# One product for values and ranks' scores, another layout of the dispatch table, and an earlier sum of the last chunk

## The chip, the cores and the metric

The kernel runs on one core of a Trainium2 chip. The metric is the time of one execution on the device in microseconds (us). The kernel before was run three times: 2809.46, 2814.0 and 2821.68 us, median 2814.0. One further execution was profiled.

The engines are TensorE (PE: matmuls, with weight loads listed apart as PEld), VectorE (DVE), ScalarE (ACT), GpSimd (POOL) and SyncE (SP), which issues most of the DMAs. GpSimd issues the indirect ones.

## The reference, cut to what matters

The input has 8 x 256 = 2048 tokens of 512 numbers, all in float32. Two layers follow each other:

```python
xn = _layernorm(x)
x = x + _L0_attn_ref(xn, ...) + _L0_ffn_ref(xn, ...)
xn = _layernorm(x)
x = x + _L1_attn_ref(xn, ...) + _L1_ffn_ref(xn, ...)
```

- `_L0_attn_ref` is linear attention with decay: 32 heads of 128, silu on queries, keys and values, causal within each sequence of 256. The heads' outputs are normalised together by their root mean square over all 32 x 128 numbers of a token, scaled by `norm_w`, multiplied by a sigmoid gate and projected to 512.
- `_L0_ffn_ref` is a mixture of 16 experts of width 128. A router picks two groups of four experts and then two experts for each token. A shared expert of width 256 is added for every token.
- `_L1_attn_ref` is softmax attention with a single head of 128: `q, k, v = x @ Wqkv + bqkv`, then a projection `Wo` with bias.
- `_L1_ffn_ref` is a low-rank mixture: `scores = x @ Wr.T` over 64 adapters of rank 16, the top 16 kept with softmax gates, `h = A x`, each rank multiplied by its adapter's gate, then `B h`, scaled by 2.

## The kernel before, in words

**Tiling.** Tokens are worked on in NCH = 4 chunks of CH = 512, each of TPC = 4 tiles of P = 128 tokens. The 512 channels are NC = 4 blocks of 128 partitions. Transposed operands have channels on the partitions. Every matmul here is in float32, and the profile counts two TensorE records for one. The large products use a seven-product scheme for 2x2 blocks in place of eight; the names `p1` to `p7` are its products.

**Opening.** Chunk by chunk, tokens are normalised (`Normal`, L251 to L258), transposed on TensorE (`turn_rows`, L278), and multiplied with the shared expert's weights (`shared_up`, L357). In `shared_up` a call of `between()` after each of the four projections computes the router's scores of one tile (`scores`, L313, 16 columns). Then `route` picks the experts on VectorE. Once all chunks are routed, the dispatch (L523 to L571) works out for each token and each of its two experts a slot number: the experts' tokens stand in NMT = 47 tiles of 128 slots, each tile belonging to one expert. `slots` holds the slot numbers, `own_` and `rows_` the expert of each tile.

**First layer.** Three loops: chunk i, group g (8 groups of four heads), and the outer product p in the order p1, p2, p6, p5, p3, p7, p4. Each outer product has seven inner ones of four matmuls (`product`, L731), 49 inner products in a group, and a group takes about 73 us. After each inner product `slot()` runs what is due of a list of `pieces`, such as scores of attention, projections and experts; `later(n, f)` puts a piece n slots ahead. ScalarE and GpSimd keep the program's order here; the other engines' instructions are ordered by the framework's planner, which takes the earliest in the program among those that its own model of the chip holds for ready. `tc.keep_in_program_order(ins)` pins an instruction behind all that its engine was given before. In chunk 0 weights are summed for the seven products: raw blocks are loaded (`st`, L674, from the pool `stage` of two buffers, tag `xw`) and added on VectorE and GpSimd, and the sums are stored in `ws` (L694). Later chunks load them (L705 to L708). For p1, p2 and p4 (`RAW`) block 0 of the weights is loaded as well, but `sums_of` uses only blocks 1 to 7.

**Experts.** In chunk 0 `scatter` (L1194) writes each token's number, 16 times in 64 bytes, to its slot of `table` in DRAM. In the last group of chunk 0, after 4 slots, `read_table` (L1203) loads the table into a buffer of `stage` with 47 partitions, one for each tile of slots. `turn_table`, 36 slots later, picks every 16th number, turns 47x128 to 128x47 on TensorE and writes `whose`. From chunk 1 on, `Expert(j)` gathers by column j of `whose` the tokens of tile j.

**Sums of squares.** `attend` adds the squares of two heads side by side into `sums` (two halves of S = 256 columns per sequence) on GpSimd. At a chunk's end `done` takes the column sums over partitions with matmuls against `ones` (`squares`, L1033): two for each tile, one for each half. `means` gives the factor `all_rms`; `finish` (L642) adds the attention's accumulator times this factor to the residual sum on VectorE. For chunks 0 to 2 this residual (shared expert and input, `xr`, with the experts' bias added by `last_bias` on GpSimd) is loaded by `load_sum`, and the result is stored in `xs_` by `store`.

**Second layer.** Before it begins, `wrapped_up` adds chunk 0's expert outputs (`gather`, L604, and `settle`, L615). Its loop over i runs two `low_rank` calls (L1601, seven products each) and one seven-product scheme with `B` (L1701). Python lists under the keys 1, 2, 7, 5, 3, 4 (`fill1`, `fill2`, `fill`) say which other work follows which product. In `fill1` and `fill2` the next chunk's sum is loaded (`next_x`), settled and normalised. In `fill` the next chunk's `Head` works: `route` (ranks, L1457, 64 columns, then the choice of 16 on VectorE), `qk` (L1453), `values` (L1520, 128 columns), `softmax` and `gates`. `gates` stores the chosen gates in DRAM, and `spread` (L1572) loads them back, repeated for each rank. Chunk 0's `Head` has an opening of its own, which puts the ranks between the matmuls of queries and keys (L1457, L1476). For chunk 3, `next_x` loads `xr` itself, adds the bias on GpSimd, and the third iteration (i = 2) runs `finish` in `fill1` under keys 2 and 7. A tile of the second layer that is asked for with `spare8()` comes from the pool `stage`.

## Time and profile before

| | |
|---|---|
| median of 3 runs | 2814.0 us (2809.46 to 2821.68) |
| the profiled execution | 2815.0 us |
| its span, first to last instruction | 2813.1 us |
| mean granted TensorE clock | 0.993 of full |
| TensorE busy | 2752.4 us, 98% of the span |
| VectorE, ScalarE, GpSimd busy | 1630.7, 947.6, 1645.8 us |
| moved by DMA | 752.66 MB, mean 268 GB/s |

A line of a timeline gives start and duration in us, engine, line of the kernel, operation, output<-inputs and shape; in brackets stands how long the engine was idle before and what it waited for. A line of waits gives the total in us, how many times, and the longest. A line of the chain (the work that ended last, followed back) gives start, duration and what ran. Engines with a q (SPq) are the issuing sides. Lines with L100 come from a helper for all additions, so tile names tell them apart. TensorE's granted clock falls to 0.5 of full at times. By the trace the first chunk of the first layer begins near 120 us and ends near 707, the later ones take about 585 us each, and the second layer begins near 2507.

### The profile page before, as it was taken

The page shows a single profiled execution, that of the slowest core. Times are in us where ns is not written, and L with a number is a line of the kernel's source. Part 1 is how long each engine was busy: PE and PEld are TensorE (multiplying, and loading weights), DVE is VectorE, ACT ScalarE, POOL GpSimd, SP SyncE. Part 2 cuts the span into 40 slices and gives each one's busy share as a digit, 9 for nine tenths or more (in the row PEclk, how much of TensorE's full clock was granted, in tenths as well). Part 3 has the DMA queues.
Part 4 walks back from the last instruction along what each step waited for, and adds up shares of the span by engine and source line. Part 5 has one row for each costly group of instructions (what it writes and reads, how often), then busy time and mean ns, then how long its engine had stood idle before and what let it go on. Part 6 is the DMA issues. An engine that isn't in the chain of part 4 may idle for free.

```text
span 2813.1 us, 49529 instructions
## 1 busy us (share of the span) xinstructions
PE 2752.4 (98%) x19653; PEld 2538.8 (90%) x19653; DVE 1630.7 (58%) x2722; ACT 947.6 (34%) x1683; POOL 1645.8 (59%) x1414
## 2 busy tenths in 40 slices
PE   9999999998999999999999999999999999999999
PEld 5699999998989999999999999999999999987877
DVE  7666777776445555555545555555455555656663
ACT  4232222221433333333343333333433333432211
POOL 6467777775566676666755555556555567642220
PEclk9999999999999999999999999999999999999999
DMA  7888888887977877778877777787777788662211
GB/s 276 322 339 337 319 330 329 322 317 293 346 273 288 290 288 273 288 277 299 316 264 261 261 271 261 264 311 279 282 271 265 270 312 305 221 222 77 68 55 62
DMA packets 155062, 752.66 MB, mean 268 GB/s; under 512 B 18721, under 2 KB 25249, under 8 KB 103457
## 3 DMA queue, kind: packets, MB, share of 16 engines
q1 hardware_dynamic: 136672, 678.67, 64.7%
q0 software_dynamic: 17872, 70.32, 7.6%
q8 instruction: 155, 2.54, 0.3%
q14 instruction: 75, 0.61, 0.1%
q10 hardware_dynamic: 288, 0.52, 0.1%
HBM read 605.66 MB, written 142.99 MB: 266 GB/s over the span
## 4 chain that ended last, share of the span: by engine, by line
PE 85%; DVE 6%; DMA 4%; issue 2%; POOL 2%; ACT 1%; another core or an unknown queue 0%; SPq 0%; DVEq 0%; POOLq 0%; ACTq 0%
PE ps_a L731 25%; PE ps_e L731 12%; PE ps_sc L942 10%; PE ps_b L731 7%; PE ps_o L865 4%; PE ps_sc L962 3%; PE ps_sc L853 3%; PE ps_sc L800 3%; PE ps_a L1601 2%; PE ps_o L866 2%; PE ps_sc L854 2%; PE ps_a L1701 2%; DMA st<-in_w_att_dram 2%; DVE w L100 1%; PE ps_sc L812 1%
## 5 line engine op out<-in xcount | busy, mean ns | idle before, releaser
L731 PE MATMUL ps_a<-xt,w 128*128 128x128 f32 x5376 | 752.9, 276 | 17.2 <-DVE r L100 7.8
L731 PEld LDWEIGHTS ps_a<-xt,w 128*128 128x128 f32 x5376 | 687.8, 192 | 47.3 <-issue 14.1
L100 POOL TENSOR_TENSOR c<-c 128x512 f32<-128x512 f32 x240 | 305.5, 1288 | 268.9 <-DVE c L100 266.5
L1099 ACT COPY cp<-ps_a 128x512 f32<-128x512 f32 x384 | 224.3, 584 | 667.7 <-PE ps_a L731 642.3
L100 POOL TENSOR_TENSOR c<-c,r 128x512 f32<-128x512 f32 x264 | 346.3, 1334 | 166.7 <-DVE r L100 164.2
L731 PE MATMUL ps_e<-xt,w 128*128 128x128 f32 x2688 | 374.8, 276 | 5.2 <-DVE c L100 1.6
L100 POOL TENSOR_TENSOR w<-w 128x512 f32<-128x512 f32 x224 | 298.2, 1339 | 93.2 <-DVE w L100 44.7
L731 PEld LDWEIGHTS ps_e<-xt,w 128*128 128x128 f32 x2688 | 341.3, 192 | 12.1 <-issue 4.8
L731 PE MATMUL ps_a<-w,xt 128*128 128x128 f32 x1792 | 346.9, 275 | 0.0
L100 POOL TENSOR_TENSOR sums<-sums,sq 128x512 f32<-128x512 f32 x120 | 155.9, 1299 | 280.9 <-ACT sq L880 280.4
L942 PE MATMUL ps_sc<-wo,gT 128*128 128x256 f32 x1288 | 304.9, 380 | 2.4 <-POOL gT L100 2.4
L731 PEld LDWEIGHTS ps_a<-w,xt 128*128 128x128 f32 x1792 | 272.6, 192 | 0.0
L942 PEld LDWEIGHTS ps_sc<-wo,gT 128*128 128x128 f32 x1288 | 232.9, 190 | 30.5 <-issue 2.9
L100 DVE TENSOR_TENSOR acc<-ps_sc,acc 128x512 f32<-128x512 f32 x208 | 142.6, 689 | 192.6 <-PE ps_sc L942 151.1
L885 DVE SCALAR_TENSOR_TENSOR gT<-ps_o,nw,c 128x256 f32<-128x256 f32 x256 | 111.9, 478 | 214.9 <-ACT sq L880 205.9
L731 PE MATMUL ps_b<-xt,w 128*128 128x128 f32 x1536 | 216.0, 277 | 13.1 <-DVE w L100 6.2
L100 DVE TENSOR_TENSOR c<-ps_a,c 128x512 f32<-128x512 f32 x216 | 146.8, 687 | 123.3 <-PE ps_a L731 118.5
L731 PEld LDWEIGHTS ps_b<-xt,w 128*128 128x128 f32 x1536 | 196.1, 194 | 16.0 <-issue 12.6
L828 ACT ACTIVATE c<-c 128x512 f32<-128x512 f32 x256 | 150.4, 628 | 145.8 <-DVE c L100 127.0
L880 ACT ACTIVATE sq<-ps_o 128x512 f32<-128x512 f32 x120 | 71.7, 597 | 367.0 <-PE ps_o L866 359.5
L100 DVE TENSOR_TENSOR s<-ps_sc,decay 128x384 f32<-128x384 f32 x256 | 139.5, 553 | 81.5 <-PE ps_sc L854 76.8
L731 PE MATMUL ps_e<-w,xt 128*128 128x128 f32 x896 | 173.5, 275 | 0.0
(306 smaller groups left out, 4747.4 us busy)
## 6 DMA issues: line engine op xcount, KB each, us to landing
w<-in_w_att_dram SPq DMA_DIRECT2D x128, 1024.0 KB
st<-in_w_att_dram SPq DMA_DIRECT2D x32, 1024.0 KB
wo<-in_w_out_dram SPq DMA_DIRECT2D x113, 256.0 KB
decay<-dec SPq DMA_DIRECT2D x64, 384.0 KB
w<-ws0p SPq DMA_DIRECT2D x12, 1792.0 KB
w<-ws1p SPq DMA_DIRECT2D x12, 1792.0 KB
w<-ws2p SPq DMA_DIRECT2D x12, 1792.0 KB
w<-ws3p SPq DMA_DIRECT2D x12, 1792.0 KB
```

Of the source, the lines that this page charges most:

```text
L100: (eng or nc.vector).tensor_tensor(o, a, b, op)
L731: mm(bank[:, bass.ts(ty, P)], a, b, start=(first and ty == 0), stop=True, skip_group_check=True,)
L800: mm(pu[:, bass.ts(n, P)], w12[:, n, c, :], self.xeT[:, c, :], start=(c == 0), stop=(c == NC - 1),)
L828: nc.scalar.activation(qk, qk, AF.Silu)
L853: mm(p[:, 0:S], self.c[:, 2 * hh, P : 2 * P], q, start=True, stop=True)
L854: mm(p[:, S : S + P], self.c[:, 2 * hh + 1, P : 2 * P], q[:, 1, :], start=True, stop=True,)
L865: mm(po[:, bass.ts(hh, S)], v[:, 0, :], self.s[:, hh, 0:S], start=True, stop=False)
L880: nc.scalar.activation(sq, po, AF.Square)
L885: nc.vector.scalar_tensor_tensor(gT[:, h, :].rearrange("p (t n) -> p t n", t=2), po[:, bass.ts(h, S)].rearrange("p (t n) -> p t n", t=2), ...
L942: mm(py[:, bass.ts(t, S)], self.O[p][:, hh, bass.ts(t, P)], self.wo[p][:, hh, :], start=(t == 0 and hh == 0), stop=(hh == 1), skip_group_c ...
L962: mm(py[:, bass.ts(h, S)], gT[:, hh, bass.ts(t, P)], self.wo[pair, h][:, hh, :], start=(h == 0 and hh == 0), stop=(hh == 1), skip_group_ch ...
L1099: nc.scalar.copy(c, bank)
```

## The change

- **Values and scores.** `fr` is joined to `wqkv` on the host. `Head.route` computes values (128 columns) and ranks' scores (64) as one product of 192 columns, in two halves of two tiles, each with a PSUM bank of its own. `values`, `opening` and `choose` go; chunk 0's head runs `route`, then `qk`.
- **Table by partitions.** A slot s is stored at row (s mod 128) * 47 + s / 128 (`places`, three VectorE operations in the dispatch), so that a partition's entries lie together. `read_table` reads 32 columns and later 15, into the buffer `sq`; `take_table` copies each half to `whose` 40 slots after its read, and starts the second read. The transpose goes. Both reads are pinned on SyncE's queue.
- **Squares.** In a chunk's last group GpSimd adds the two halves of `sums`; `squares` runs one matmul for a tile.
- **Last chunk's sum.** In i = 0, chunk 3's `xr` is loaded, gets its bias and its `finish` (without the pin), and is stored in `xs_`. `next_x` then loads `xs_` for every chunk.
- **Smaller parts.** In the second layer's `fill`, two of the next chunk's four `turn_rows` stand after the first product. RAW loads of later chunks take blocks 1 to 3. In the opening, the first of each tile's score matmuls of chunk 0 is pinned behind the projection before it.

```diff
-    def scores(pl, xT, t):
+    def scores(pl, xT, t, kept=lambda ins: ins):
         for c in range(NC):
-            mm(
+            ins = mm(
...
+            if c == 0:
+                kept(ins)
...
-        ups.append(shared_up(i, lambda: scores(pl, xT[i], tiles.pop(0))))
+        ups.append(shared_up(i, lambda: scores(pl, xT[i], tiles.pop(0), lambda ins: tc.keep_in_program_order(ins) if i == 0 else ins)))
...
+    whose = [const.tile([P, n], I32, name=f"whose{n}") for n in (READ, NMT - READ)]
...
+    nc.vector.tensor_scalar(tile_of, slots, 7, None, ALU.arith_shift_right)
+    nc.vector.tensor_scalar(places, slots, P - 1, None, ALU.bitwise_and)
+    nc.vector.scalar_tensor_tensor(places, places, float(NMT), tile_of, ALU.mult, ALU.add)
...
-                nc.sync.dma_start(out=y, in_=w_att[g, RAW[p]])
+                nc.sync.dma_start(out=w[:, 1:4], in_=w_att[g, RAW[p]][:, 1:4])
...
+                if u.g == NG - 1 and self.pair == 1:
+                    add(sums[:, 0:S], sums[:, 0:S], sums[:, S:], nc.gpsimd)
...
-                        for n in range(2):
-                            mm(
-                                pr[:, t : t + 1],
-                                sums_[i][:, t // 2, n * S + t % 2 * P : n * S + (t % 2 + 1) * P], ones,
-                                start=(n == 0), stop=(n == 1),
-                            )
+                        mm(
+                            pr[:, t : t + 1], sums_[i][:, t // 2, bass.ts(t % 2, P)], ones,
+                            start=True, stop=True,
+                        )
...
-                out_offset=bass.IndirectOffsetOnAxis(ap=slots[:, n, t : t + 1], axis=0),
+                out_offset=bass.IndirectOffsetOnAxis(ap=places[:, n, t : t + 1], axis=0),
...
-        def read_table():
-
-            rows = staged("rows")[0:NMT, 0 : P * SAME]
-            nc.sync.dma_start(out=rows, in_=table.rearrange("(j p) o -> j (p o)", p=P).bitcast(FP))
...
+        def read_table(n=0):
+
+            m = min(READ, NMT - n * READ) * SAME
+            rows = attn.tile([P, CH], FP, tag="sq", name="rows")[:, 0:m]
+            lo = n * READ * SAME
+            tc.keep_in_program_order(
+                nc.sync.dma_start(
+                    out=rows, in_=table.rearrange("(p j) o -> p (j o)", p=P)[:, lo : lo + m].bitcast(FP)
+                )
+            )
+
+            def take_table():
                 tc.keep_in_program_order(
                     nc.vector.tensor_copy(
-                        byno[0:NMT], rows.bitcast(I32).rearrange("j (p o) -> j p o", o=SAME)[:, :, 0]
+                        whose[n], rows.bitcast(I32).rearrange("p (j o) -> p j o", o=SAME)[:, :, 0]
                     )
                 )
-                pt = ps_sc()
-                nc.tensor.transpose(pt[:, 0:NMT], byno[0:NMT, :], ident[0:NMT, 0:NMT])
-                nc.vector.tensor_copy(whose, pt[:, 0:NMT])
-
-            later(36, turn_table)
+                if n == 0:
+                    read_table(1)
+
+            later(40, take_table)
...
-        if i + 1 < NCH:
-            nc.sync.dma_start(out=x_, in_=xs_[i])
-        else:
-            nc.sync.dma_start(out=x_, in_=xr[i])
-            last_bias(x_, work.tile([P, C], FP, tag="sb3", name="sb3", bufs=1))
+        nc.sync.dma_start(out=x_, in_=xs_[i])
...
         def route(self):
...
+            for h in range(2):
+                pv = ps_sc()
+                for t in range(2 * h, 2 * h + 2):
+                    for c in range(NC):
+                        mm(
+                            pv[:, bass.ts(t % 2, n)], self.yT[:, c, bass.ts(t, P)], wqkv_t[:, c, 2 * P :],
+                            start=(c == 0), stop=(c == NC - 1),
+                        )
+                pv = pv[:, 0 : 2 * n].rearrange("p (t d) -> p t d", t=2)
+                nc.vector.tensor_copy(sc[:, bass.ts(h, 2), :], pv[:, :, P:])
+                tt(self.v[:, bass.ts(h, 2), :], pv[:, :, 0:P], bv_t.to_broadcast([P, 2, P]), ALU.add)
...
-    head.opening()
-    head.values()
+    head.route()
+    head.qk()
     head.softmax()
...
-            if i + 2 == NCH:
-                for k, ns in ((2, (0, 1)), (7, (2, 3))):
-                    fill1[k].append(partial(finish, i + 1, following[0], ns, tc.keep_in_program_order))
...
-            for t in range(TPC):
-                turn_rows(yT1, settled[i + 1], t, ps_sc())
...
+            turned(0)
+            turned(1)
             head = Head(i + 1)
-            fill = {2: [fourth, head.route], 7: [head.qk], 5: [head.values], 3: [head.softmax], 4: [head.gates]}
+            fill = {1: [partial(turned, 2), partial(turned, 3)], 2: [fourth, head.route], 7: [head.qk], 3: [head.softmax], 4: [head.gates]}
+        if i == 0:
+
+            x3 = spare8()
+            nc.sync.dma_start(out=x3, in_=xr[NCH - 1])
+            last_bias(x3, work.tile([P, C], FP, tag="sb3", name="sb3", bufs=1))
+            fill[4].append(partial(finish, NCH - 1, x3))
         seven(work, product, AB, XB, out_, fill)
+        if i == 0:
+            nc.sync.dma_start(out=xs_[NCH - 1], in_=x3)
```

## The prediction

> **What bounds the kernel now.** I read the page's busy shares first, then the waits of TensorE, then stretches of time, then the timelines of the stretches that lose time.
>
> ```profile
> PE   2752.4 (98%) x19653; PEld 2538.8 (90%) x19653; DVE 1630.7 (58%) x2722; ACT 947.6 (34%) x1683; POOL 1645.8 (59%) x1414
> ```
>
> TensorE is busy for 2752.4 of 2813.1 us. So time comes back in two ways only: fewer or cheaper matmuls, or one of the few places where TensorE stands still or runs at half clock. From the waits of TensorE (total, times, longest):
>
> ```profile
> PE ps_b L731 <- DVE w L100: 6.2, 1, 6.2
> PE ps_sc L278 <- DVE spare L258: 4.1, 4, 2.2
> PE ps_e L1601 <- DVE cp L100: 3.8, 1, 3.8
> PE ps_sc L1554 <- DVE v L100: 2.2, 1, 2.2
> ```
>
> Each is a place that the diff touches. The first is in the last group of chunk 0. SyncE's timeline there, one group earlier (two lines) and in the last group (three):
>
> ```profile
> 571.90 0.33 SPq L674 DMA_DIRECT2D st<-in_w_att_dram  x1
> 587.09 0.43 SPq L674 DMA_DIRECT2D st<-in_w_att_dram  x1
> ...
> 646.12 0.30 SPq L1203 DMA_DIRECT2D rows<-table  x1
> ...
> 652.14 0.33 SPq L674 DMA_DIRECT2D st<-in_w_att_dram  x1
> ...
> 674.38 0.33 SPq L674 DMA_DIRECT2D st<-in_w_att_dram  x1
> ```
>
> From the group's first `st` pair (557.02 and 631.54) the p5 block is issued after 14.9 us in the ordinary group and after 20.6 us in the last, the p7 block after 30.1 and 42.8. `rows` sits in one of the two `staged` buffers from 646.12 until its reader at 700.3, and `st` needs them. The cost on TensorE (timeline, then chain):
>
> ```profile
> 653.41 1.16 PE L731 MATMUL ps_b<-xt,w 128*128 128x128 f32 x4 [2.03 <-issue]
> 673.85 1.62 PE L731 MATMUL ps_b<-xt,w 128*128 128x128 f32 x6 [6.21 <-DVE w L100]
> ```
> ```profile
> 673.85 3.69 PE ps_b L731 x16
> 678.19 1.79 PE ps_a L731 x16
> ```
>
> Sixteen matmuls take 3.69 us after the gap and 1.79 us later: half clock. The same happens in the second layer's third iteration (i = 2), where the `finish` of chunk 3 waits for GpSimd's bias:
>
> ```profile
> 2680.36 5.83 POOL L100 TENSOR_TENSOR x<-x,sb 128x512 f32<-128x512 f32 x4 [19.20 <-DVE pT L1624]
> 2688.72 3.78 PE L1601 MATMUL ps_e<-t,fa 128*128 128x256 f32 x8 [3.78 <-DVE cp L100]
> 2692.30 3.04 PE L1601 MATMUL ps_a<-wsm,fa 128*128 128x256 f32 x8
> 2695.18 1.89 PE L1601 MATMUL ps_b<-wsm,fa 128*128 128x256 f32 x8
> ```
>
> The price list for the merged product, from the chain: 32 ranks, 32 values, 16 matmuls of 256 columns, and the squares.
>
> ```profile
> 2638.40 3.52 PE ps_sc L1457 x32
> 2641.91 3.51 PE ps_a L1701 x16
> 2659.20 3.57 PE ps_sc L1520 x32
> 2505.35 1.69 PE ps_sc L1033 x16
> ```
>
> **What the Trainium skill says.** "TensorE: Matmul & The Clock Gate", LDWEIGHTS (loading the stationary operand), has a weight load cost by its columns whatever is streamed: some 107 ns for 128. The trace agrees: 0.110 us a matmul at 64 columns, 0.106 at 1, 0.112 at 128, but 0.216 at 256. Part 1 of the same page says that the clock halves after an idle window of about 3.4 us and needs a busy one to return. The granted clock agrees: 0.50 in the stretches 674 to 676 and 14 to 22 us. "SBUF — State Buffer", SBUF: two separate sides, makes the port pair of VectorE and GpSimd an exclusive lock; the `finish` operations took 1242 ns on average beside GpSimd's bias in i = 2, and `settle`, of the same shape, 744 ns.
>
> **The change part by part.** The sum is against the profiled execution's own 2815.0 us (span 2813.1 plus 1.9 around it), which stands 1.0 us above the median of 2814.0.
>
> 1. Values and scores as one product. Per chunk it removes 32 matmuls of 64 columns (3.52 us) and 32 of 128 (3.57), and adds 32 of 192. Where streaming sets the pace, 3.51/16/256 gives 0.86 ns a column; 192 columns take 0.165 us, 32 of them 5.3 us. Saved 3.52 + 3.57 - 5.3 = 1.8 us, four chunks: **-7.2**. VectorE's copies and bias adds are halved in size and doubled in number, in stretches where it has idle time (9.17 us of it before 2587.79).
>
> 2. Squares. Eight of 16 matmuls of 0.106 us go: 0.85 us a chunk, **-3.4**. In their place GpSimd adds 128x256 twice a chunk, some 0.73 us each (between its 0.46 for 128x128 and 1.27 for 128x512). In chunk 3 the squares start at 2505.19, 2.8 us after the sums ended at 2502.41, so it is covered. At 1346.8, where `gT` is queued behind the sums and TensorE waits 1.23 us for it, it isn't: **+0.7**.
>
> 3. The table. The read moves to the `sq` buffer, which chunk 0 doesn't use, so `st` gets its buffer back. Gone: the gaps 2.03 and 6.21, and half of the half-clock time that TensorE worked (653.4 to 657.0 and 673.9 to 677.5: 3.6 us each, 1.8 lost each): 11.8. An ordinary group keeps some 0.8 us of gaps, so **-11.0**. The transpose (two matmul slots at most) and its bank give **-0.3**. Three VectorE operations of 128x32 are added in the dispatch, where VectorE has no gap and TensorE waits (1.83 and 1.62 us): the cast of the same shape took 0.18 us, chained some 0.15: **+0.5**. Both reads are pinned on SyncE's queue; the second waits for the first's copy on VectorE, and behind it stand the weight loads of chunk 1. That copy falls due at the 45th of the group's 49 slots, near the 700.3 us of today's reader; those loads start at 712.16. I take 0; the cost is up to 5 if SyncE gets there early. The last scatter was issued at 624.4 and landed some 6 us later, so the first read waits for nothing.
>
> 4. Chunk 3's sum. From i = 2 go four bias adds, four `finish`, and the stall: 3.78 us of gap, and 6.6 us for 16 matmuls that otherwise take 3.46: **-6.9**. In i = 0 the same work returns with one more 1 MB load and one more 1 MB store on SyncE. GpSimd stands idle from 2523 to 2549 and VectorE for 5.9 us between 2530 and 2537.6, which hides 4 x 0.74 us. If it falls into 2540 to 2560 instead, where VectorE is busy 19.5 of 20 us, all 3 us cost, and 5 with the lock. The new tile also takes the `staged` buffer into which chunk 2's sum is loaded at 2482 today; that load now waits for a release, and its first use is at 2611. I take **+1.0** (0 to 7).
>
> 5. The second layer's start. VectorE stands idle for 10.04 us until all ranks are done, then chooses, and TensorE waits 2.22 us behind it. With the product in two halves and queries and keys after it, choosing runs under 6.9 us of matmuls: **-2.2**.
>
> 6. Transposes between two products. TensorE waits 2.17, 0.57, then 0.52 + 0.84 us for `scaled`. Two of the four now stand after p1. The trace shows the planner already putting p1 ahead of all four, so the move alone may give nothing; but VectorE's backlog shrinks by parts 4 and 5. Between 0 and -4.1: **-2.0**.
>
> 7. RAW weight loads shrink by 256 KB, 72 times, 18.9 of 752.7 MB. TensorE waits for weights 2.7 us in all (1.3, 1.1, 0.3); 0 to -2.7: **-1.0**.
>
> 8. Router scores of chunk 0 pinned behind the projections. The 16 at 12.92 run at half clock and stand before the first projection, which runs at half clock to 22.66. Starting with the dense product should bring the clock back one window (3.4 us) sooner, worth 1.7 us at most; if the shared weights aren't there by 13 us, up to 3.5 us are lost. **-0.3**.
>
> Sum: -7.2 -3.4 +0.7 -11.0 -0.3 +0.5 -6.9 +1.0 -2.2 -2.0 -1.0 -0.3 = -32.1, so 2782.9 for this execution, **2782** for a median.
>
> **The rivals.** A: the table's stall only moves. SyncE is held by a pinned read, or the second `st` is late anyway because one DMA engine lags (23 to 28 GB/s from 668 to 674). For it: that lag, which I can't explain. Against: `st` at 652.14 waited for a buffer. It gives part 3 back: 2793. B: the work put into i = 0 costs there what it saved in i = 2, by chunk 2's late load, on which VectorE's pinned `settle` waits. Against: 60 us of room. 2789 to 2793. C, slower: SyncE reaches the second read a whole 40-slot delay early (about 58 us at 73 us for 49 slots), so the weight stream stops. Weights are loaded two outer products ahead, which covers some 20 us (73/7 each); TensorE would lose up to 38 us, 2820. It becomes slower than before once SyncE is held more than 20 + 32 = 52 us, and slower by over 0.5% only with two such stops or other losses beside it, some 2830. Against: loads wait for TensorE's buffers, so SyncE rarely runs that far ahead.
>
> **How the numbers follow.** A change of 0.5%, 14 us, is about what a measurement of this kernel can tell from none. Forecast 0.70 (2770 to 2792); A 0.10; B 0.10; both A and B, or other losses by the planner's new order, 0.06 (2800 to 2815); C 0.04. The lower end adds what parts 6, 7 and 8 may still give (2.1 + 1.7 + 1.4) and the full 11.8 and part 4 free: about 2774, less a little for an ordering that helps, 2770. The upper end takes in A and B singly, with the 5 of a held queue: 2799. Faster below 2800: 0.89; within 0.5%: 0.07; slower: 0.04.
>
> **What would show it.** Part 3: no TensorE gap over 2 us between 640 and 690, `st` issued as in other groups, clock 1.00. Part 1: 32 matmuls in about 5.2 us, no line of 64 columns. Part 4: no gap near the later 2685, VectorE's `finish` of chunk 3 before the second iteration. Part 5: no wait for `v` or its successor. Wrong would be a long wait of SyncE at the table's reads, a VectorE wait for chunk 2's sum, or a half-clock stretch that isn't there now.

## The result, and the profile after

The changed kernel takes 2781.6 us (median of 4 runs, 2779.2 to 2786.4), the kernel before beside it 2815.3 us (2809.5 to 2821.7): ratio 0.9882, 95% interval 0.9856 to 0.9908. The profiled execution has a span of 2778.5 us against 2813.1, so 34.6 us went.

The page of the changed kernel, busy times:

```profile
PE 2733.5 (98%) x19492; PEld 2522.7 (91%) x19492; DVE 1627.6 (59%) x2733; ACT 947.2 (34%) x1683; POOL 1649.8 (59%) x1422
```

TensorE's busy time fell by 18.9 us, its time at rest by some 15.7 (34.6 - 18.9). Its waits after (total, times, longest), those in the places of the change:

```profile
PE ps_sc L278 <- DVE spare L258: 2.8, 4, 0.8
PE ps_sc L948 <- POOL gT L100: 2.8, 2, 1.6
...
PE ps_sc L1598 <- DVE pb L1526: 2.2, 1, 2.2
```

The waits of 6.2 us (table), 3.8 (third iteration) and 2.2 for `v` are gone, the transposes' wait (L278) fell from 4.1 to 2.8. But a wait of 2.2 us is back under another name: TensorE now waits for the softmax's `pb`.

A ledger shows where the time went. Each row is a stretch between two points in TensorE's timeline that both kernels have (the first outer product, boundaries of groups, the first of the squares' matmuls, the first matmul with `B` of an iteration). The forecast is put together from the prediction's terms.

| stretch | before | after | change | forecast |
|---|---|---|---|---|
| opening, to the first outer product | 121.0 | 119.9 | -1.2 | +0.2 |
| chunk 0, groups 1 to 7 | 480.7 | 479.4 | -1.2 | 0 |
| chunk 0, last group | 82.1 | 73.7 | -8.4 | -11.3 |
| chunk 1, first two groups | 151.9 | 147.1 | -4.8 | -1.0 |
| from there to chunk 3's squares | 1669.5 | 1664.0 | -5.5 | -1.9 |
| to `B` of i = 0 | 48.3 | 48.9 | +0.6 | -3.9 |
| to `B` of i = 1 | 75.2 | 71.7 | -3.5 | -2.5 |
| to `B` of i = 2 | 80.4 | 71.5 | -8.8 | -9.4 |
| to `B` of i = 3 | 74.3 | 72.6 | -1.7 | -2.5 |
| rest | 29.8 | 29.7 | -0.1 | 0 |

The sum was forecast at 32.1 (the rows are rounded) and came to 34.6. Row by row it's less good: the start of the second layer gave nothing where 3.9 us were expected, and the first layer's later groups gave 10.3 where 2.9 were.

The prices of the chain, after, hold: the 32 merged matmuls take 5.20 us (forecast 5.3; before 3.52 + 3.57), and eight squares 0.80 us (before 16 in 1.69).

```profile
2484.28 0.80 PE ps_sc L1038 x8
...
2542.86 5.20 PE ps_sc L1468 x32
```

SyncE's timeline in the last group of chunk 0, after:

```profile
632.44 0.46 SPq L1210 DMA_DIRECT2D rows<-table  x1
...
643.21 0.33 SPq L678 DMA_DIRECT2D st<-in_w_att_dram  x1
...
657.18 0.42 SPq L678 DMA_DIRECT2D st<-in_w_att_dram  x1
```

From the group's `st` pair (629.76) the p5 block follows after 13.5 us and the p7 block after 27.4; before it was 20.6 and 42.8. The timeline there, VectorE and TensorE:

```profile
647.64 1.56 DVE L100 TENSOR_TENSOR w<-w,st 128x512 f32<-128x512 f32 x1
649.12 0.68 DVE L100 TENSOR_TENSOR acc<-ps_sc,acc 128x512 f32<-128x512 f32 x1
649.73 0.68 DVE L100 TENSOR_TENSOR c<-ps_b,cp 128x512 f32<-128x512 f32 x1
```
```profile
650.50 0.68 PE L735 MATMUL ps_b<-xt,w 128*128 128x128 f32 x4 [2.03 <-issue]
```

The first of the two gaps, 2.03 us, is still there. The profile names no releaser ("issue"), but TensorE starts at 650.50, just when VectorE has read the bank `ps_b` (649.73 to 650.41), and VectorE comes to that late, behind the sums of p6's weights. So I take the gap to be VectorE's; the table's new buffer and layout left it as it was.

### The profile page after: what moved, and what is told of

Same layout as the page of the kernel before. It is cut to its first block, busy times and chain, and to the rows that moved or that the text cites. A ratio compares the mean times of both kernels' runs of the same rounds, so it can differ in the third digit from the quotient of the medians.

```text
span 2778.5 us, 49222 instructions
## 1 busy us (share of the span) xinstructions
PE 2733.5 (98%) x19492; PEld 2522.7 (91%) x19492; DVE 1627.6 (59%) x2733; ACT 947.2 (34%) x1683; POOL 1649.8 (59%) x1422
## 4 chain that ended last, share of the span: by engine, by line
PE 86%; DVE 6%; POOL 3%; issue 3%; DMA 2%; ACT 0%; SPq 0%; DVEq 0%; POOLq 0%; ACTq 0%
PE ps_a L735 25%; PE ps_e L735 13%; PE ps_sc L948 10%; PE ps_b L735 7%; PE ps_sc L968 4%; PE ps_o L869 4%; PE ps_sc L857 3%; PE ps_sc L804 3%; PE ps_o L870 2%; PE ps_sc L858 2%; PE ps_a L1676 2%; PE ps_sc L816 1%; DVE w L100 1%; PE ps_a L1579 1%; PE ps_a L359 1%
## 5 line engine op out<-in xcount | busy, mean ns | idle before, releaser
L884 ACT ACTIVATE sq<-ps_o 128x512 f32<-128x512 f32 x120 | 71.7, 597 | 358.1 <-PE ps_o L870 352.7
```

The source lines that it names most:

```text
L884: nc.scalar.activation(sq, po, AF.Square)
```

## The experiments

Twelve kernels were run, each beside the kernel before; ratios are to that. How far one execution can be trusted is seen in the last group of chunk 0. Four kernels whose TensorE order in the first layer is the same (the changed one, and those below with the late sum, without bo, and with the gates on ScalarE) took 73.7, 71.5, 74.1 and 76.8 us for it, and two more of that order, bias_early_kept and loads_late, 77.1 and 71.5. Most of that is the clock. Each has a gap of 1.7 to 2.0 us near 650, and two of them (gates_act, bias_early_kept) another of about 2 us just before. Here are the same 12 us of sum_late, of the changed kernel and of gates_act (PE, PEld, DVE, ACT and POOL busy, then TensorE's clock, DMA share, GB/s):

```profile
646.00:658.00 12.00, 10.34 (x80) 9.59 (x79) 9.53 (x14) 3.40 (x6) 9.18 (x7) 1.00 0.76 283
646.00:658.00 12.00, 9.97 (x67) 9.33 (x66) 7.90 (x13) 2.49 (x5) 8.81 (x8) 0.86 0.79 302
646.00:658.00 12.00, 8.18 (x42) 7.56 (x41) 7.62 (x10) 0.32 (x1) 8.81 (x7) 0.72 0.65 236
```

A clock of 0.86 over 12 us is a half clock of 3.4 us, 0.72 one of nearly 6.8, 1.00 none. The same gap of 2.03 us is followed by a half clock in the changed kernel and by none in raw_full. In the changed kernel's trace, the half-clock stretches that begin at 126.24, 651.89 and 2505.33 us lie 525.65 and 1853.44 us apart, that is 154 and 543 times 3.413 us, and each lasts 3.413 us. By these figures the half clock comes and goes at fixed steps of 3.413 us, so I infer that what a gap of some 2 us costs depends on how it falls between them. The first group of chunk 2 scatters likewise (74.3 to 74.7 us in seven executions with the changed kernel's order there, 76.5 to 76.8 in three that have a half clock near 1330), and so does the stretch to `B` of i = 3 (72.5 to 76.0). So a span differs by a few us by chance, and the readings below go by stretches. From chunk 3's squares to `B` of i = 2 the changed kernel needs 192.1 us (203.9 before).

| kernel | ratio, 95% interval | span | last group of chunk 0 | squares of chunk 3 to `B` of i = 2 |
|---|---|---|---|---|
| changed | 0.9882 (0.9856 to 0.9908) | 2778.5 | 73.7 | 192.1 |
| rows_staged | 0.9884 (0.9867 to 0.9902) | 2778.9 | 74.6 | 192.8 |
| rows_48 | 0.9961 (0.9942 to 0.9979) | 2804.7 | 72.9 | 203.0 |
| table_alone | 0.9949 (0.9933 to 0.9966) | 2798.7 | 71.5 | 202.5 |
| sum_late | 0.9900 (0.9882 to 0.9917) | 2781.2 | 71.5 | 197.1 |
| no_bo0 | 0.9897 (0.9880 to 0.9913) | 2777.6 | 74.1 | 193.1 |
| gates_act | 0.9877 (0.9860 to 0.9894) | 2784.9 | 76.8 | 192.1 |
| bias_early | 0.9902 (0.9880 to 0.9924) | 2786.2 | 74.1 | 197.8 |
| bias_early_kept | 0.9897 (0.9874 to 0.9921) | 2784.2 | 77.1 | 195.9 |
| loads_late | 0.9891 (0.9875 to 0.9907) | 2776.8 | 71.5 | 191.8 |
| raw_full | 0.9906 (0.9889 to 0.9922) | 2785.2 | 72.4 | 191.1 |
| apart | 0.9907 (0.9885 to 0.9929) | 2786.4 | 74.5 | 197.1 |
| unpin | 0.9887 (0.9866 to 0.9907) | 2781.5 | 74.5 | 191.6 |

### The table: buffer, or shape of the read?

**rows_staged**, the first read back in the staged buffer:

```diff
-            rows = attn.tile([P, CH], FP, tag="sq", name="rows")[:, 0:m]
+            rows = staged("rows")[:, 0:m] if n == 0 else attn.tile([P, CH], FP, tag="sq", name="rows")[:, 0:m]
```

> The changed kernel, with the first read of the table put back into one of the two staged buffers; its layout by partitions, its two halves and its delay stay. If the buffer was the cause of the 6.21 us wait at 673.85 (my reading in part 3), the second st block of the last group waits for a release again: a TensorE gap of 5 to 7 us near 670 and a second half-clock stretch, 7 to 9 us slower than the changed kernel, about 2789; the first gap (2.03 us, there in both kernels) stays as it is. If rival A holds, that a lagging transfer and not the buffer made the wait, which the other layout happened to cure, the time is that of the changed kernel, 2782 within 2. A further 4 to 5 us would come if the gain in chunk 1's first groups hangs on the same buffer: 2794.

SyncE's timeline:

```profile
644.13 0.33 SPq L1210 DMA_DIRECT2D rows<-table  x1
...
650.15 0.33 SPq L678 DMA_DIRECT2D st<-in_w_att_dram  x1
...
661.33 0.33 SPq L678 DMA_DIRECT2D st<-in_w_att_dram  x1
```

The buffer is held from 644.13 until its reader at 695.07, and the p5 block is late as it was before (650.15 against 652.14). Yet VectorE has it at 658.53, the p7 block goes out at 661.33 instead of 674.38, and the 6.21 us gap does not return: ratio 0.9884, the changed kernel's. The buffer theory of the prediction's part 3 falls. Back to the kernel before, then, to VectorE's timeline and to stretches (columns as above):

```profile
671.85 2.50 DVE L100 TENSOR_TENSOR w<-w,st 128x512 f32<-128x512 f32 x4 [9.30 <-DMA st<-in_w_att_dram]
```
```profile
662.00:668.00 6.00, 5.64 (x35) 5.02 (x33) 0.55 (x1) 0.00 (x0) 0.00 (x0) 1.00 0.78 332
668.00:674.00 6.00, 0.15 (x1) 0.18 (x2) 2.15 (x4) 0.00 (x0) 0.12 (x1) 0.71 0.06 26
```

VectorE waits 9.30 us for a block whose load was issued at 652.14, almost 20 us earlier. In the last 6 us the DMAs move 26 GB/s with 0.06 of 16 engines busy: one engine. The trace's single packets agree: from 667.88 to 671.29 packets of 8 KB follow one by one with nothing beside them but records of 4 bytes, and then come 8 of 3 KB and twice 8 of 2 KB, just a sixteenth of the loads of `decay` and `wo` that were issued behind `st`. So the load was late in its transfer and not in its issue. The Trainium skill, "DMA: Bandwidth & Descriptors", section "Why a DMA increments its semaphore by 16 and not by 1", says how many engines share a copy: the largest number up to 16 that divides the slowest dimension of both its patterns. For 47 rows that's 1. In the trace a packet of 8 KB takes 0.31 us, so 47 of them hold one engine for 14.6 us, and the share of `st` on that engine stands behind them.

**rows_48** tests it in the kernel before, with one row of padding and nothing else (in the trace the matmuls have the same order, but for swaps of neighbours between 130 and 150 us, and VectorE, ScalarE and GpSimd do the same work in the same order):

```diff
-    table = dram.tile([NSLOT, SAME], I32, name="table")
+    table = dram.tile([NROW * P, SAME], I32, name="table")
...
-            rows = staged("rows")[0:NMT, 0 : P * SAME]
+            rows = staged("rows")[0:NROW, 0 : P * SAME]
```

> The kernel before, with one row more in the table, so that its read is 48 rows of 8 KB into 48 partitions instead of 47; buffer, place, layout and transpose stay as before. New theory: a read of 47 rows cannot be shared evenly by 16 DMA engines and goes to one of them, 47 packets of 0.31 us = 14.6 us, while 48 rows give each engine three. Then the st block behind it lands some 10 us after its issue and no longer 20, VectorE's wait of 9.30 us at 671.85, TensorE's wait of 6.21 us and the half clock after it are gone: 8 to 9 us faster than the kernel before, about 2804, though the staged buffer is still held. Rival, the buffer (already weakened by the run with the rows staged): no change, the 6.21 us wait stays, 2812 to 2814. Second rival: a slow DMA engine for a reason that has nothing to do with the table; no change either.

Its SyncE timeline and the same stretches:

```profile
646.87 0.34 SPq L1203 DMA_DIRECT2D rows<-table  x1
...
665.86 0.33 SPq L674 DMA_DIRECT2D st<-in_w_att_dram  x1
```
```profile
668.00:674.00 6.00, 6.00 (x53) 5.92 (x52) 6.00 (x9) 0.00 (x0) 4.56 (x4) 1.00 0.40 156
```

The p7 block goes out 8.5 us earlier, the 6.21 us gap and the half clock behind it are gone (TensorE busy for all of 668 to 674), and the last group takes 72.9 us instead of 82.1. The whole is 11 us faster (ratio 0.9961) and the span 8.4 us shorter, with buffer, place, layout and transpose as before. The span gains less than the last group, since the group before it took 71.9 us instead of 68.5 in this execution, with a wait of 1.74 us for VectorE's `s` and a half clock behind it, such as gates_act and bias_early_kept have in the last group. So the number of rows made the stall. The gap near 652 stays (1.87 us). That one DMA engine was behind with its share is seen in the packets. That it was this one because it carried all 47 rows is what the skill's rule and rows_48 say; the packets carry no engine's number, so that isn't seen directly.

**table_alone**, the table's part of the change put into the kernel before:

> The kernel before with the table's part of the change alone (places by partitions, two reads into the sq buffer, no transpose, three more VectorE operations in the dispatch). The forecast had -11.0, -0.3 and +0.5, so -10.8. If the 6.21 us wait and its half clock alone go, -8 to -9. If the gain of a further 4.8 us that the changed kernel shows between its 8th and 10th group (chunk 1's first two) belongs to the table's part too (the experts' first loads or the weight stream start sooner), that stretch gets 4 to 5 us shorter here and the whole is -12 to -14, about 2800; if it comes from the smaller loads of part 7, that stretch stays as before.

Ratio 0.9949, so -14.4 us; the last group takes 71.5 us (no half clock follows its gap near 650), and chunk 1's first two groups 149.6 instead of 151.9. Of the 4.8 us won there 2.3 belong to the table's part, though not to the row count, for rows_48 needs 152.2. Since its order of matmuls differs in places, I can't say what in the part does it.

### The last chunk's sum

**sum_late**, with `next_x`, the pinned `finish` in `fill1` and the end of the loop as before:

```diff
-        if i == 0:
-            x3 = spare8()
...
+            if i + 2 == NCH:
+                for k, ns in ((2, (0, 1)), (7, (2, 3))):
+                    fill1[k].append(partial(finish, i + 1, following[0], ns, tc.keep_in_program_order))
```

> The changed kernel, with chunk 3's sum made in the second layer's third iteration again, as before. Theory: the gap of about 3.8 us and the half clock after it come back there (near 2690) and nothing is gained back in the first iteration, because the sum's bias, finish and store cost nothing there: 6 to 8 us slower than the changed kernel, about 2789. Rival B: the sum costs as much in the first iteration as it saved in the third; then the first iteration gets 2 to 7 us shorter here and the whole is within 2 us of the changed kernel. A third outcome: the stall in the third iteration was tied to other work and does not come back, so the time does not move and the iteration stays as in the changed kernel.

The timeline of the third iteration, GpSimd and TensorE:

```profile
2650.76 5.83 POOL L100 TENSOR_TENSOR x<-x,sb 128x512 f32<-128x512 f32 x4 [15.72 <-DVE pT L1606]
```
```profile
2659.12 3.68 PE L1583 MATMUL ps_e<-t,fa 128*128 128x256 f32 x8 [3.79 <-DVE cp L100]
```

The gap is back with its half clock (eight matmuls in 3.68 us), and the third iteration takes 77.3 us instead of 71.5: +5.8. In the first iteration the sum's absence gives 1.3 us (47.6 against 48.9), of which some may be chance: rows_staged, unpin and raw_full, with the changed kernel's second layer, took 49.0, 48.4 and 48.0. Net to `B` of i = 2 it's 5.0 us, where the forecast had 5.9.

### The second layer's start

Here the changed kernel gained nothing. Its timeline, GpSimd, VectorE and TensorE:

```profile
2496.02 4.93 POOL L100 TENSOR_TENSOR spare<-spare,wob 128x512 f32<-128x512 f32 x4
```
```profile
2496.74 4.27 DVE L1494 TENSOR_SCALAR G<-G,tot 128x64 f32<-128x64 f32 x1
```
```profile
2505.49 0.45 PE L1598 MATMUL ps_sc<-ident,pb 128*128 128x128 f32 x1 [2.20 <-DVE pb L1526]
```

A scaling of 128x64, which took 0.24 us at 2491.48, takes 4.27 us and ends at 2501.01, just as GpSimd's four additions of `bo` end (2500.95). The Trainium skill, "SBUF — State Buffer", section "SBUF: two separate sides", calls the two engines' port pair an exclusive lock; the trace agrees, and shows that a whole run of GpSimd operations can keep it. The softmax's maxima queue behind the scaling, and TensorE waits for them 2.20 us, then works at half clock for 3.4 us.

**no_bo0**, which leaves `bo` out of chunk 0's output:

```diff
-            add(xc[:, t, :], xc[:, t, :], bo_t, nc.gpsimd)
+            if i:
+                add(xc[:, t, :], xc[:, t, :], bo_t, nc.gpsimd)
```

> The changed kernel without adding the output bias bo to chunk 0 (its four GpSimd additions of 128x512 in the second layer's first iteration are left out, so that chunk's output lacks bo). Theory: these additions hold the port pair that VectorE and GpSimd share, while VectorE's scaling of the gates waits 4.27 us at 2496.74, and the softmax behind it makes TensorE wait 2.20 us and run at half clock for 3.4 us. Without them the scaling takes about 0.1 to 0.25 us, the 2.20 us gap and the half clock after it go: 3 to 4 us faster than the changed kernel, about 2778. Rival: the choosing itself is the late work (a chain of 36 VectorE operations before the softmax's maxima); then the scaling gets short but the gap at the softmax stays at 1.5 us or more, and the time moves by less than 1 us.

**gates_act**:

```diff
-                nc.vector.tensor_scalar(self.G[:, t, :], self.G[:, t, :], tot, SCALING, ALU.mult, ALU.mult)
+                nc.scalar.mul(self.G[:, t, :], self.G[:, t, :], tot)
...
-            nc.scalar.copy(GT, pg[0:K, :])
+            nc.scalar.mul(GT, pg[0:K, :], SCALING)
```

> The changed kernel with the scaling of the gates done by ScalarE (four small operations a chunk, the factor 2 put into ScalarE's copy of the turned gates), the additions of bo left where they are. If the lock of the shared port pair is what delays VectorE in front of the softmax, an operation of ScalarE is not held by it and the softmax's maxima, read from PSUM, follow at once: 2 to 4 us faster than the changed kernel, about 2779. If VectorE's next operation from SBUF to SBUF (the softmax's own scaling) is held by the same additions instead, the wait only moves: within 1 us. In chunks 1 to 3 I expect nothing either way.

Without `bo` the scaling takes 0.26 us and the softmax's wait falls to 0.18, as the lock theory had it. But the time doesn't fall. The next three lines are of no_bo0's timeline, of GpSimd, VectorE and TensorE:

```profile
2505.96 5.82 POOL L100 TENSOR_TENSOR spare<-spare,sb 128x512 f32<-128x512 f32 x4 [11.92 <-DMA sb<-in_b_dram]
```
```profile
2507.25 1.73 DVE L646 SCALAR_TENSOR_TENSOR spare<-acc,rms,spare 128x512 f32<-128x512 f32 x1 [6.25 <-POOL spare L100]
```
```profile
2509.64 2.08 PE L1614 MATMUL ps_o<-pT,v 128*128 128x256 f32 x4 [5.14 <-DVE pT L1602]
```

The row of bias for chunk 3's sum lands at 2505.96 only, GpSimd waits for it, `finish` waits for GpSimd, and the planner had put `finish` ahead of the copies `pT` on VectorE. TensorE waits 5.14 us. So the sum moved by part 4 does stand in the way at i = 0. In the changed kernel the same row lands at 2507.86 and the same `finish` stands ahead of the first `pT`, but TensorE, held up by the softmax, has no wait for it. With the gates on ScalarE the hold passes to VectorE's next operation that reads SBUF:

```profile
2499.70 5.96 DVE L100 TENSOR_TENSOR wsm<-wsm 128x512 f32<-128x512 f32 x1 [1.62 <-PE ps_sc L1457]
```

It ends at 2505.66, just after the additions of `bo` (2500.16 to 2505.10); in the changed kernel it took 0.68 us, behind the scaling. TensorE then waits 3.02 us in place of 2.20, and the second layer is no faster. The lock is shown, and so is that removing the operation it catches gains nothing.

**bias_early** (chunk 3's load and bias at the end of the first layer, `bo` of chunk 0 after the product), **bias_early_kept** (and chunk 2's load pinned behind the gates' loads) and **loads_late** (and 2.5 MB of other transfers behind the first of them) were meant to be better than the changed kernel (the diff shows the first one's load and bias, and the last one's order of loads and store):

```diff
         while pieces:
             pieces.pop(0)[2]()
+        x3 = spare8()
+        nc.sync.dma_start(out=x3, in_=xr[NCH - 1])
+        last_bias(x3, attn.tile([P, C], FP, tag="sum", name="sb3", bufs=3))
...
         low_rank(0, fill1)
+        if i == 0:
+            behind.pop()(tc.keep_in_program_order)
+            tc.keep_in_program_order(nc.sync.dma_start(out=xs_[NCH - 1], in_=x3))
```

> A version meant to be better than the changed kernel: chunk 3's sum and its bias row are loaded at the end of the first layer, GpSimd adds the bias there, ahead of the gathers, and bo of chunk 0 is added after the attention's product instead of before it. Theory: neither the additions of bo (lock, 4.27 us) nor the wait of VectorE's finish for GpSimd's bias stands any longer between the ranks and the softmax; the waits of 0.45, 0.30, 0.33 and 2.20 us and the half clock after them go: 3 to 5 us faster than the changed kernel, about 2777. Rival: GpSimd's four bias additions now meet VectorE's choosing and hold the lock there, and the choosing ends as late as before: within 1 us of the changed kernel.

> The run with the bias early lost its gain to SyncE: the load of chunk 2's sum had been put ahead of the eight loads of the spread gates and waited there for a buffer, 7.71 us of TensorE's time. Here chunk 3's sum is finished and stored at the very start of the second layer, and the load of chunk 2's sum is pinned behind the spread gates. Theory: the 7.71 us wait and the half clock after it (some 9 us) go and nothing else changes: 2777 to 2779 in the profile, that is 3 us under the changed kernel, or a little less if the later additions of bo delay the normalisation (the waits at the transposes were 2.1 us there against 0.73). Rival: the store of chunk 3's sum now stands ahead of the load of chunk 1's sum on SyncE, and the settle of chunk 1 waits for it; then a wait of some microseconds near 2515 takes its place and the time stays at 2781 or more.

> The two runs with the bias early showed what stands behind the softmax at the start of the second layer: the gates are stored and read back (spread over the partitions) through DMA queues that carry some 6.5 MB of loads issued from 2486 on at about 410 GB/s, until about 2510, and the products wait for the spread gates. Here, beside the early bias and the later bo, 1.5 MB of that (the three sums of fb, which the second low-rank product needs only after 2533) and the 1 MB store of chunk 3's sum stand behind the first spread gates. Theory: the gates land by about 2507 and the spread gates by 2511, the wait of 5.39 us and the half clock after it go: 2776 to 2778 in the profile, 3 to 4 us faster than the changed kernel. Rival: the delayed 2.5 MB now stand in front of the second four spread gates and of chunk 2's sum, and the second half of the low-rank product waits instead, 2 to 5 us: 2780 to 2783, no better than the changed kernel.

bias_early has no TensorE gap over 0.25 us from the squares to 2518, and then SyncE and TensorE:

```profile
2512.37 0.33 SPq L1446 DMA_DIRECT2D spare<-xs  x1
2512.79 15.63 SPq L1553 DMA_DIRECT2D spread_g<-gd  x8
```
```profile
2526.06 3.50 PE L1582 MATMUL ps_e<-wsm,fa 128*128 128x256 f32 x8 [7.71 <-DVE cp L100]
```

The load of chunk 2's sum stood ahead of the gates' loads and was issued at 2512.37 only, though SyncE had been free since 2503.7. Pinning it behind them left a wait of 5.39 us: the gates are stored at 2504.10, and the first load of them goes out 9 us later, at 2513.06, while the DMAs move 366 to 426 GB/s from 2494 to 2510 with the loads of the layer's operands. So chunk 2's load hadn't held the gates for most of that time; the operands' loads were the next suspect. With 2.5 MB of these put off, the gates are loaded from 2504.25 on and `B` of i = 0 begins 45.7 us after the squares instead of 48.9. Then i = 1 takes 74.6 us instead of 71.7, with waits of 1.63 and 1.44 us at the transposes. The other two have that as well (73.3 and 73.9 us), so the later `bo`, which all three share, may be its cause; no run parts that. Net nothing, ratio 0.9891. Each of the three lost elsewhere what it gained, or more.

### Three single parts

**raw_full**, all four blocks loaded again:

```diff
-                nc.sync.dma_start(out=w[:, 1:4], in_=w_att[g, RAW[p]][:, 1:4])
+                nc.sync.dma_start(out=y, in_=w_att[g, RAW[p]])
```

> The changed kernel with all four blocks of a RAW weight loaded again, 256 KB more in each of 72 loads. The forecast had 1.0 us for this part (0 to 2.7). The trace of the changed kernel lacks five small waits of chunks 1 to 3 that the kernel before had (groups 8 to 10, 11, 13, 28 and at the squares), some 4 us beside the first groups' gain. If the smaller loads did that, they come back: 3 to 5 us slower than the changed kernel, 2784 to 2786, and up to 9 if the first groups' 4.8 us is theirs as well. If those waits went for other reasons (the order of the instructions, the squares), the time is within 1 us of the changed kernel.

Ratio 0.9906: 6.8 us slower than the changed kernel, though the intervals of the two overlap; the span is 6.7 us longer. Chunk 1's first two groups take 149.1 us instead of 147.1, and from there to chunk 3's squares it's 1669.4 instead of 1664.0. But no wait of TensorE for a load is in the trace after 690. Its rests grew by 1.4 us from 770 to 2500, mostly for VectorE's and GpSimd's results; what is left of the difference is no wait that it lists. Group by group, 2.4 us of the 5.4 lie in the first group of chunk 2 (77.0 against 74.6 us), where a half clock stands that gates_act, loads_late and unpin have as well, so that is chance. Without it the part is worth about 5 us: 2.0 in chunk 1's first two groups and 2.9 in three others. With the longer loads the planner gave TensorE another order in places (from 711 to 770 us and near 1380 and 1970), so these 5 us are load and order together; they were not parted.

**apart**, values and ranks as two products in the same places:

```diff
+                    for lo, m in ((P, K), (0, P)):
...
-                            pv[:, bass.ts(t % 2, n)], self.yT[:, c, bass.ts(t, P)], wqkv_t[:, c, 2 * P :],
+                                pv[:, at : at + m], self.yT[:, c, bass.ts(t, P)],
+                                wqkv_t[:, c, 2 * P + lo : 2 * P + lo + m],
```

> The changed kernel with values and ranks as two products again (64 and 128 columns), in the same places, halves and banks as the merged one. The prices of the chain say 32 of 64 columns 3.52 us, 32 of 128 columns 3.57 us, and 32 of 192 took 5.20 to 5.28 us: 1.85 us a chunk, 7.4 us in all, 2788. If the weight load sets the pace of all three and the stationary operands could be kept, or if the saving was hidden by VectorE's choosing, which follows the product, less than 4 us.

From its chain (64 matmuls):

```profile
2543.52 7.14 PE ps_sc L1470 x64
```

7.14 against 5.20 us is 1.94 a chunk, and the whole is 7.0 us slower by the ratios, whose intervals overlap. By stretches, to `B` of i = 1, 2 and 3 it costs 3.2, 1.9 and 3.4 us, and to `B` of i = 0 nothing (48.6 against 48.9). The third can't be told from chance: unpin, whose second layer is the changed kernel's, took the same 76.0 us there. In chunk 0, as I read it, the merged product only made TensorE come earlier to the softmax's wait.

**unpin**:

> The changed kernel without the pin of chunk 0's router scores behind the projections. The forecast had 0.3 us for the pin; the trace of the changed kernel shows a half clock of 3.4 us instead of 10.2 at the start, and the first product 1.2 us earlier. If the pin did that, the half clock is 10 us long again and the first product is 1.2 to 1.6 us later, with the same loss at the end: 2782 to 2783, which the profile can show and the times hardly. If the shorter half clock has another cause (transposes, the order of the loads), the opening stays as in the changed kernel.

From 12 to 20 us the clock is 0.62 and 0.53 (four us each) instead of 0.70 and 0.87, so the pin does shorten the half clock; in all ten executions with the pin the second of these stretches has 0.71 to 0.99, in the four without it 0.50 to 0.53. The first outer product comes at 118.6 us, not later than with the pin (119.9). rows_48 and table_alone have the opening of before (table_alone with three small operations more in the dispatch), whose first outer product in the profile above came at 121.0, and it comes at 119.8 and 119.9 in them. The 1.2 us in the ledger's first row are scatter; the pin is worth nothing that can be seen.

## Why the prediction was right in sum, and where it was wrong

**Part 1** (-7.2) is right in its price: 1.94 us a chunk in the chain where 1.8 were forecast. Undoing it cost 7.0 us by the ratios, 5.1 of them clear of chance by stretches; chunk 0's share was lost in the stall that followed. **Part 2** is right: eight squares take 0.80 instead of 1.69 us for 16, -3.6 in all, and the wait for `gT` rose from 1.23 to 1.65, +0.4 for the forecast's +0.7 (it is 1.46 to 2.36 in other executions).

**Part 3** (-10.8) had a fair size and a wrong reason. That `rows` sits in one of the two `staged` buffers "and `st` needs them" was read from the times of issue. The failed step is to take the second `st` (674.38) as late by its buffer, without asking when the first one, issued at 652.14, had landed: VectorE's own line said that it waited 9.30 us for that DMA. The run with the buffer taken again gives no loss, the run with 48 rows gives the gain. Rival A named the lagging engine and the 23 to 28 GB/s, but called them unexplained and concluded that the stall would stay; the read it came from was in the diff. And the first gap of 2.03 us, counted as gone, is still there, behind VectorE's queue of weight sums as I read it. The last group gave 8.4 us, or 10.6 in table_alone, where 11.3 were forecast; the 2.2 us between these two are mostly a half clock. Another 2.3 us came in chunk 1, which part 3 didn't have.

On the half clock, the prediction took an idle window of about 3.4 us for the condition and found the trace in agreement. The measurements differ, and they decide: gaps of 1.87 us (rows_48) and 2.03 (before and after) were followed by a half clock too.

**Part 4** (-6.9 + 1.0) is right: 5.8 us in the third iteration, at most 1.3 given back in the first. Rival B had its place right: in no_bo0 TensorE waits in i = 0 behind the moved work. In the changed kernel no wait for it is seen beside the softmax's stall.

**Part 5** (-2.2) is wrong. The step that failed is "choosing runs under 6.9 us of matmuls". The choosing has 36 operations on VectorE's queue in front of the softmax, and one of them was held for 4.27 us by GpSimd's additions of `bo`, which stand right behind its gathers (2496.02). The wait changed its name from `v` to `pb`, 2.22 to 2.20 us, plus 1.1 us of shorter ones, and a half clock of 3.4 us followed. With it went, as I read it, chunk 0's share of parts 1 and 2. Nor would a longer cover have been enough: no_bo0 has no such wait and is no faster. The forecast of -3.9 for this stretch became +0.6.

**Part 6** (-2.0): the waits at L278 fell by 1.3 us. The planner puts the transposes after i = 0 where it had them, and there the wait fell from 2.17 to 0.73 us; VectorE's smaller backlog, the second half of that step, would explain it, but no run tests that. The total can't be told from chance: unpin, with the same second layer, has 4.1 us of these waits, as much as the kernel before. **Part 7** (-1.0, at most 2.7) is mis-sized: about 5 us. TensorE's waits for DMAs were taken as the ceiling of what a smaller load can bring; raw_full loses those 5 us with no wait for a load in its trace. The planner's order, which changed with the loads, may be the reason; that isn't shown. **Part 8**: -0.3 was forecast, nothing is seen. **Rival C**: the second read went out at 694.72 and chunk 1's loads at 700.63, with no gap of TensorE over 0.5 us from 652 to 772.

So 32.1 against 34.6 is partly luck: about 4 us too little for part 7 and 2 for the table's gain in chunk 1, about 4.5 too much for the second layer's start.

## What to carry to other kernels

When an engine waits for a buffer's next load, look up when the load before it landed, and compare issue with landing before blaming the buffer; then look at the row counts of the transfers around it. Before counting a removed wait as won, list what is queued behind it up to the next transfer that can't come sooner: here softmax, `finish`, the gates' way through DRAM and the transposes took turns. Where a planner orders the work by its model of the chip, the waits for DMAs in a trace need not be the ceiling for what smaller loads bring.

## What the runs showed that I had not expected

- A read of 47 rows of 8 KB delayed a later 1 MB load on the same queue to almost 20 us; 48 rows, more data, made the kernel 11 us faster (ratio 0.9961).
- Four GpSimd additions of 128x512 in a row made a VectorE operation of 128x64 last 4.27 us instead of 0.24, and one of 128x512 5.96 instead of 0.68: one operation waits for the whole run of them, not for one.
- The same group of the first layer, with TensorE's instructions in the same order, took 71.5 to 77.1 us in six executions, mostly by whether a half clock of 3.4 or 6.8 us, or none, followed a gap of about 2 us.
